# Inverse square roots of all norms: one power on GpSimd in the place of Newton's steps on VectorE

## The chip, the cores and the metric

The kernel runs on one core of one Trainium2 chip. The metric is the device time of one execution in microseconds; a kernel's time is the median of its runs. A profiled execution gives a trace of every instruction on the core's engines: TensorE (PE; its weight loads are PEld), VectorE (DVE), ScalarE (ACT), GpSimd (POOL) and the queue of SyncE (SP) that issues the transfers.

## The reference

One decoder block on x of shape (8, 224, 512) in float32, with a context of shape (8, 750, 384): self-attention, cross-attention and a quantised FFN, each followed by a residual sum and a layernorm.

```python
x = layernorm(x + attn(x)); x = layernorm(x + xattn(x, ctx)); x = layernorm(x + ffn(x))

# layernorm, eps = 1e-5, no weights
(x - mean) / sqrt(var + eps)

# attn: RMS norm of x, then 16 heads of 64; q and k each normalised per head
x = x * rsqrt(mean(x * x) + eps) * norm_w
q, k, v = x @ Wq, *split(x @ Wkv)
q = q / max(norm(q), 1e-12) * (q_gamma + 1) * 8          # k in the same way
sim = tanh(q @ k.T / 50) * 50 / 8
out = softmax(sim) @ v @ Wo

# xattn: plain attention, scale 1/8, bias bo behind Wo
# ffn: rows of x and of silu(gate) * up rounded to 8 bits, weights rounded to -1, 0, 1
```

Every inverse square root in it belongs to a norm: the RMS norm (one value for each row of x), the head norms (16 values for each row: 8 heads of q and 8 of k, for one half of the heads), and the three layernorms (one value for each row).

## The kernel before

The 1792 rows of x are 14 tiles of 128 rows, which stay in SBUF (`x[i]`) and are changed in place. On TensorE, VectorE, ScalarE and GpSimd the instructions run in the order in which the code issues them; an instruction that waits holds up all that are behind it on its engine, and the engines wait for one another through semaphores.

*Self-attention* (lines 212 to 454). It runs over 64 units, one for each of 8 batches and 8 pairs of heads. A unit issues `self_scores` (scores on TensorE, L331; tanh and exponential on ScalarE, L339 and L345; the row sums of the probabilities on GpSimd, L350 and L351, tile asm), then `self_values` of the unit before (products with v, L360; the sums spread by a matmul with ones, L369; reciprocal L377 and product L379 on VectorE), then the jobs of its slot, then the layernorm of a tile whose output projection `self_finish` ended in the unit before. The jobs prepare the batch that comes next: `project_qk` (matmuls L245; ScalarE copies the result out with the RMS norm's factor, L257; GpSimd squares it, L259; VectorE sums the squares of each head, L260), `transpose_qk`, `project_v`, `transpose_xn`. With the second of q and k, `project_qk` clips the sums (L266), calls `rsqrt` on 16 columns (tile h_rs) and multiplies q and k by it (L271). `layernorm` takes the statistics of a tile (L147 to L149), calls `rsqrt` on one column (ln_rs) and normalises (L161). `transpose_xn` turns x for the next projections: TensorE L235, then VectorE L237 (tile xnT). The PSUM buffers of tag mm are four, and L237 and L287 empty them for the next transposes and projections.

*Cross-attention* (lines 516 to 900). 64 units again. VectorE subtracts the maxima (L767), ScalarE takes the exponential (L775), GpSimd adds up the rows (L777 to L779, tiles csh and csm). `cross_add` puts the result into x[i] and takes the statistics; `roots(i0, i1)` calls `rsqrt` for a range of tiles (ln_rss) at units 34 and 57, and `normalise_x` uses them from the next unit on.

*FFN* (lines 904 to 1075). Tile by tile: `gate_up` on TensorE (L922), h on VectorE (L932), quantisation of h by ScalarE, GpSimd (L965) and VectorE (L974), a transposing transfer, `contract` on TensorE (L1010, tile dn), `add` on VectorE (L1024) with statistics. `add` calls `roots` when the last tile of one of the `groups` (L1019) has been added; `store` then normalises the tiles of the group (L1036), on GpSimd inside the loop and on VectorE behind it, and sends each out. For the three tiles left over from cross-attention, `roots(NX - 3, NX)` is called at i = 1 and `normalise_x` at i = 2.

`rsqrt` (L130) takes a first guess by a shift and a subtraction on the bits of the float (L133, L136) and improves it by three of Newton's steps of three instructions each (L140 to L142): 11 VectorE instructions on a tile of 128 rows and 1 to 16 columns.

Of the kernel before, what the change touches and what calls it, by code (L numbers as in the profile page):

```python
# [20 lines left out]
F32 = mybir.dt.float32  # L21
BF16 = mybir.dt.bfloat16
AF = mybir.ActivationFunctionType
ALU = mybir.AluOpType
AX = mybir.AxisListType
I32 = mybir.dt.int32
PSUM = bass.MemoryType.PSUM
ENGINES = {
    mybir.EngineType.PE,
# [10 lines left out]
P = 128  # L40
# [3 lines left out]
NX = B * S // P  # L44
# [19 lines left out]
def decoder_block(ctx: ExitStack, tc: tile.TileContext, a: dict, out: bass.AP):  # L64
    nc = tc.nc

    const = ctx.enter_context(tc.tile_pool(name="const", bufs=1))
# [3 lines left out]
    stat = ctx.enter_context(tc.tile_pool(name="stat", bufs=4))  # L71
# [50 lines left out]
    make_identity(nc, ident)  # L122
    ident16 = const.tile([P, P], BF16, name="ident16")
    nc.vector.tensor_copy(ident16, ident)
    ones = const.tile([P, P], F32, name="ones")
    nc.gpsimd.memset(ones, 1.0)

    gscale = const.tile([P, 2, NPAIR, 1], F32, name="gscale")

    def rsqrt(y, v, tag):  # L130

        t = stat.tile(list(v.shape), F32, tag=f"rsq{tag}", name="rsq")
        nc.vector.tensor_scalar(  # L133
            t.bitcast(I32), v.bitcast(I32), 1, None, ALU.arith_shift_right
        )
        nc.vector.tensor_scalar(  # L136
            y.bitcast(I32), t.bitcast(I32), -1, 0x5F3759DF, ALU.mult, ALU.add
        )
        for _ in range(3):
            nc.vector.tensor_tensor(t, y, y, ALU.mult)  # L140
            nc.vector.scalar_tensor_tensor(t, t, -0.5, v, ALU.mult, ALU.mult)
            nc.vector.scalar_tensor_tensor(y, t, 1.5, y, ALU.add, ALU.mult)  # L142

    def statistics(y, mv, ve):

        st = stat.tile([P, 6], F32, name="ln_st")
        nc.vector.bn_stats(st, y)  # L147
        nc.vector.bn_aggr(mv, st)
        nc.vector.tensor_scalar(ve, mv[:, 1:2], LN_EPS, None, ALU.add)  # L149

    def layernorm(tiles):

        n = len(tiles)
        mv = stat.tile([P, n, 2], F32, tag=f"ln_mv{n}", name="ln_mv")
        ve = stat.tile([P, n, 1], F32, tag=f"ln_ve{n}", name="ln_ve")
        rs = stat.tile([P, n, 1], F32, tag=f"ln_rs{n}", name="ln_rs")
        for j, i in enumerate(tiles):
            statistics(x[i], mv[:, j, :], ve[:, j, :])
        rsqrt(rs[:, :, 0], ve[:, :, 0], str(n))
        for j, i in enumerate(tiles):  # L160
            nc.vector.tensor_scalar(  # L161
                x[i], x[i], mv[:, j, 0:1], rs[:, j, :], ALU.subtract, ALU.mult
            )
# [48 lines left out]
    with tc.tile_pool(name="a_sb", bufs=2) as sb, tc.tile_pool(  # L212
        name="a_mm", bufs=4, space=PSUM
    ) as ps_mm, tc.tile_pool(name="a_sc", bufs=1, space=PSUM) as ps_sc, tc.tile_pool(
        name="a_ov", bufs=2, space=PSUM
    ) as ps_ov, tc.manual_schedule(engines=ENGINES):
        xnT = {}
        rms = stat.tile([P, NX], F32, name="rms", bufs=1)
        rms_rs = stat.tile([P, NX], F32, name="rms_rs", bufs=1)
        qkT, v, raw, norms, outs = {}, {}, {}, {}, {}  # L220
# [5 lines left out]
        def rms_norms(i0, i1):  # L226
            r = rms[:, i0:i1]
            nc.vector.tensor_scalar(r, r, 1.0 / DIM, RMS_EPS, ALU.mult, ALU.add)
            rsqrt(rms_rs[:, i0:i1], r, f"rms{i0}")


        def transpose_xn(i):
# [8 lines left out]
        def project_qk(i, which, c):  # L241

            mm = ps_mm.tile([P, 512], F32, tag="mm", name="mm_qk")
            for k in range(KD):
                nc.tensor.matmul(  # L245
                    mm,
                    lhsT=xnT[i][:, k, :],
                    rhs=(wq, wk)[which][:, k, c * 512 : (c + 1) * 512],
                    start=(k == 0),
                    stop=(k == KD - 1),  # L250
                )
            if which == 0:
                norms[i, c] = stat.tile([P, HEADS, 1], F32, name="h_ss")
            hs = norms[i, c][:, :, 0]
            qk = sb.tile([P, 512], F32, name="qk", bufs=4)
            raw[i, which, c] = qk
            nc.scalar.activation(qk, mm, AF.Identity, scale=rms_rs[:, i : i + 1])  # L257
            sq = sb.tile([P, 512], F32, tag="sq_h", name="sq_h")
            nc.gpsimd.tensor_tensor(sq, qk, qk, ALU.mult)  # L259
            nc.vector.tensor_reduce(  # L260
                hs[:, which * 8 : (which + 1) * 8],
                sq.rearrange("p (h d) -> p h d", d=DH), AX.X, ALU.add,
            )
            if which == 1:

                nc.vector.tensor_scalar(hs, hs, 1e-24, None, ALU.max)  # L266
                hr = stat.tile([P, HEADS, 1], F32, name="h_rs")
                rsqrt(hr[:, :, 0], hs, "h")
                for g in range(2):
                    part = raw[i, g, c].rearrange("p (h d) -> p h d", d=DH)  # L270
                    nc.vector.tensor_tensor(  # L271
                        part, part,
                        hr[:, g * 8 : (g + 1) * 8, :].to_broadcast([P, 8, DH]),
                        ALU.mult,
                    )
# [105 lines left out]
        def block(h):  # L381

            b, c = divmod(h, 2)
            tiles = list(needs[b])
            jobs = [(8, project_qk, i, which, c) for i in tiles for which in range(2)]
            vals = [(8, project_v, i, c) for i in tiles]
            turned = [(1, transpose_qk, i, which, c) for i in tiles for which in range(2)]
            ahead = []
            if c == 1 and b + 1 < B:
                ahead = [(1, transpose_xn, i) for i in needs[b + 1]]  # L390
            if len(tiles) == 2:
                return jobs + turned[:2] + vals[:1] + ahead + vals[1:] + turned[2:]
            return jobs + vals[:1] + ahead + vals[1:] + turned
# [4 lines left out]
        for h in range(1, 2 * B):  # L398
            jobs = block(h)
            total, at = sum(j[0] for j in jobs), 0  # L400
            for j in jobs:
                n = 4 * h - 5 + 4 * (2 * at + j[0]) // (2 * total)
# [16 lines left out]
        for i in needs[0]:  # L419
            square(i)  # L420
        rms_norms(0, 2)
        nc.vector.tensor_scalar(gscale, gam, 1.0, DH**0.5, ALU.add, ALU.mult)
        squares = list(range(2, NX))
        for n, (_, f, *args) in enumerate(block(0)):
            f(*args)
            if n < 4:
                for _ in range((1, 1, 2, 1)[n]):
                    square(squares.pop(0))
        rms_norms(2, NX // 2)
        oT = sb.tile([P, NPAIR, 2 * S], F32, name="oT", bufs=1)  # L430
        last, due = None, []
# [20 lines left out]
        for i in completes[B - 1]:  # L452
            self_finish(i)
        layernorm(due)


# [16 lines left out]
    ln_ve = const.tile([P, NX, 1], F32, name="ln_ves")  # L473
    ln_rs = const.tile([P, NX, 1], F32, name="ln_rss")
# [4 lines left out]
    xqTs = {}  # L479

    def roots(i0, i1):
        rsqrt(ln_rs[:, i0:i1, 0], ln_ve[:, i0:i1, 0], f"c{i0}")

    def normalise_x(i):

# [30 lines left out]
    with tc.tile_pool(name="c_sb", bufs=2, reuse_waits="tile") as sb, tc.tile_pool(  # L516
        name="c_mm", bufs=7, space=PSUM, reuse_waits="tile"
    ) as ps_mm, tc.tile_pool(
        name="c_ov", bufs=1, space=PSUM, reuse_waits="tile"
# [304 lines left out]
        for n, i0, i1 in ((4 * NPAIR + 2, 0, 7), (7 * NPAIR + 1, 7, NX - 3)):  # L824
            norm_at[n] = (roots, i0, i1)
            for i in range(i0, i1):
                norm_at[n + 1 + i - i0] = (normalise_x, i)
            norm_at[n + 1 + i1 - i0] = (row_scales, i0, i1)
# [75 lines left out]
    with tc.tile_pool(name="f_sb", bufs=2, reuse_waits="tile") as sb, tc.tile_pool(  # L904
        name="f_mm", bufs=6, space=PSUM, reuse_waits="tile"
    ) as ps_mm, tc.tile_pool(
        name="f_dn", bufs=2, space=PSUM, reuse_waits="tile"
    ) as ps_dn, tc.manual_schedule(engines=ENGINES):
        hs, mhs, hqs, dns, deqs = {}, {}, {}, {}, {}
        NC = HID // 512  # L910
        END = NX - 1
# [104 lines left out]
                )  # L1016


        groups = ((0, 6), (6, 9), (9, 12), (12, NX))  # L1019
        ready = []  # L1020

        def add(i):
            _, deq = deqs.pop(i)
            nc.vector.scalar_tensor_tensor(  # L1024
                x[i], dns.pop(i), deq, x[i], ALU.mult, ALU.add
            )
            statistics(x[i], ln_mv[:, i, :], ln_ve[:, i, :])
            for i0, i1 in groups:
                if i == i1 - 1:
                    roots(i0, i1)  # L1030
                    ready.extend(range(i0, i1))
# [13 lines left out]
        for i in range(NX):  # L1045
            for c in range(NC):
                gate_up(i, c)
                if c == 0 and i + 2 < NX:
                    quantise_x(i + 2)
                if c == 1 and i - LAG - 1 >= 0:  # L1050
                    add(i - LAG - 1)
                if c == 2 and i >= 1:
                    round_h(i - 1)
                    quantise_h(i - 1)
                    store(nc.gpsimd, 3 if i > 10 else 2)
            scale_h(i)
            if i - LAG >= 0:
                contract(i - LAG)
            if i == 1:
                roots(NX - 3, NX)  # L1060
            if i == 2:
                for t in range(NX - 3, NX):
                    normalise_x(t)
                row_scales(NX - 3, NX)
# [56 lines left out]
```

## Time and profile before

| what | us |
|---|---|
| runs: median of 3 (lowest, highest) | 1777.36 (1776.96, 1780.74) |
| the profiled execution | 1775.66 |
| its span, first to last instruction | 1773.8 |
| TensorE busy | 1744.9 |
| VectorE busy | 1285.6 |
| ScalarE busy | 853.4 |
| GpSimd busy | 618.1 |
| VectorE in `rsqrt`: 0 to 620 us, 620 to 1620, 1620 to the end | 99.6, 9.5, 10.1 |

Self-attention takes the first 596 us of the span, cross-attention lasts to about 1616 us, the FFN to the end. In a line of the timeline the columns are start and duration in us, engine, line of the code, operation, the tile written and the tiles read, the form, and how many instructions were merged; in brackets stands how long the engine was idle before it and what ended that. In a group of the page the numbers behind the bar are busy time in us and the mean of one instruction in ns, then the idle time before them and its releasers.

### The profile page before, as it was taken

The numbers are of one execution on the slowest core, as the hardware profiler recorded it, in microseconds if no ns is written. First come the engines' busy times: TensorE is split into PE (matmuls) and PEld (weight loads), VectorE is DVE, ScalarE is ACT, GpSimd is POOL, SyncE is SP. The second block draws the span as 40 slices with busy tenths as digits, with TensorE's granted clock in tenths as the row PEclk, the third lists the DMA queues.
The fourth block names the chain that finished last, engine by engine and source line by source line (L and its number), as shares of the span: only waits on it lengthen the run. The fifth ranks groups of instructions, "written<-read, shape, count | busy, mean of one in ns | idle before, by whom it ended". The sixth has DMA issues, their size and how long they took to land.

```text
span 1773.8 us, 24390 instructions
## 1 busy us (share of the span) xinstructions
PE 1744.9 (98%) x8994; PEld 1097.4 (62%) x8994; DVE 1285.6 (72%) x2868; ACT 853.4 (48%) x1408; POOL 618.1 (35%) x611
## 2 busy tenths in 40 slices
PE   8999999999999999999999999999999999999997
PEld 4544445444444677777677677677777776774443
DVE  4757666666666477777688688698776776986988
ACT  3344333233344266465466466365444454445663
POOL 2322322222323144344344344344434244443143
PEclk9999999999999999999999999999999999999999
DMA  7000000000004222220122112011000000031443
GB/s 279 1 1 0 1 1 1 1 1 1 1 1 145 96 72 98 72 72 33 37 66 68 45 64 84 15 42 39 1 1 30 4 1 27 1 122 43 74 81 99
DMA packets 60967, 80.52 MB, mean 45 GB/s; under 512 B 36784, under 2 KB 36784, under 8 KB 58416
## 3 DMA queue, kind: packets, MB, share of 16 engines
q1 hardware_dynamic: 60848, 78.97, 14.1%
q8 instruction: 71, 1.16, 0.3%
q14 instruction: 48, 0.39, 0.1%
HBM read 60.34 MB, written 9.96 MB: 40 GB/s over the span
## 4 chain that ended last, share of the span: by engine, by line
PE 86%; DVE 10%; issue 2%; ACT 1%; POOL 1%; DMA 1%; SPq 0%; DVEq 0%; POOLq 0%; ACTq 0%
PE mm_k L654 13%; PE mm_v L642 13%; PE mm_qk L245 11%; PE sc_c L691 8%; PE ov_c L787 8%; PE mm_o L201 5%; PE mm_co L201 5%; PE mm_q L667 5%; PE mm_f L922 4%; PE mm_v L298 3%; PE sc_a L331 3%; PE ov_a L360 2%; PE dn L1010 2%; PE ov_a L369 1%; PE tr_qk L281 1%
## 5 line engine op out<-in xcount | busy, mean ns | idle before, releaser
L777 POOL TENSOR_TENSOR csh<-cpT 125x672 f32<-125x672 f32 x128 | 207.2, 1619 | 605.5 <-DVE cpT L767 586.5
L775 ACT ACTIVATE cpT<-cpT 125x1344 f32<-125x1344 f32 x128 | 169.7, 1327 | 235.6 <-DVE cpT L767 226.9
L642 PE MATMUL mm_v<-xattn_Wv,cT 128*125 128x256 f32 x1152 | 259.1, 379 | 0.0
L654 PE MATMUL mm_k<-cT,xattn_Wk 128*128 128x375 f32 x768 | 258.6, 486 | 0.3 <-DMA cT<-ctxT 0.3
L642 PEld LDWEIGHTS mm_v<-xattn_Wv,cT 128*125 128x125 f32 x1152 | 216.3, 188 | 28.8
L699 ACT COPY cpT<-sc_c 125x448 f32<-125x448 f32 x384 | 173.9, 560 | 101.6 <-PE sc_c L691 101.3
L654 PEld LDWEIGHTS mm_k<-cT,xattn_Wk 128*128 128x128 f32 x768 | 140.0, 189 | 99.9 <-issue 12.8
L767 DVE TENSOR_TENSOR cpT<-cpT,mx_b 125x1344 f32<-125x1344 f32 x128 | 193.2, 1550 | 2.2
L701 DVE TENSOR_TENSOR cm<-sc_c,cpT 125x448 f32<-125x448 f32 x128 | 74.0, 620 | 138.4 <-ACT cpT L699 138.2
L691 PE MATMUL sc_c<-cqT,ckT 64*125 64x224 f32 x1536 | 164.3, 358 | 0.8 <-DVE cqT L675 0.7
L787 PE MATMUL ov_c<-cpT,cv 125*64 125x224 f32 x1536 | 159.4, 357 | 0.0
L691 PEld LDWEIGHTS sc_c<-cqT,ckT 64*125 64x125 f32 x1536 | 140.8, 184 | 26.4 <-ACT ckT L661 14.1
L787 PEld LDWEIGHTS ov_c<-cpT,cv 125*64 125x64 f32 x1536 | 104.6, 137 | 47.3 <-issue 18.2
L350 POOL COPY asm<-pr 32x448 f32<-32x448 f32 x64 | 35.8, 559 | 274.1 <-ACT pr L345 264.7
L260 DVE TENSOR_REDUCE h_ss<-sq_h 128x8 f32<-128x512 f32 x56 | 38.3, 684 | 121.7 <-POOL sq_h L259 121.7
L377 DVE RECIPROCAL rc_a<-ov_a 128x224 f32<-128x224 f32 x64 | 99.3, 1552 | 35.1 <-PE ov_a L369 35.1
L661 ACT COPY ckT<-mm_k 128x375 f32<-128x375 f32 x128 | 59.3, 464 | 124.1 <-PE mm_k L654 124.1
L339 ACT ACTIVATE pr<-sc_a 128x448 f32<-128x448 f32 (+1 forms) x128 | 62.2, 538 | 106.3 <-PE sc_a L331 105.8
L257 ACT ACTIVATE qk<-mm_qk,rms_rs 128x512 f32<-128x512 f32 x56 | 38.5, 688 | 153.7 <-PE mm_qk L245 150.7
L667 PE MATMUL mm_q<-xT,xattn_Wq 128*128 128x224 f32 x512 | 107.1, 352 | 0.0
L667 PEld LDWEIGHTS mm_q<-xT,xattn_Wq 128*128 128x128 f32 x512 | 96.7, 189 | 16.3
L245 PE MATMUL mm_qk<-wq,xnT 128*128 128x512 f32 x224 | 105.4, 614 | 0.8 <-DVE xnT L237 0.6
(140 smaller groups left out, 2855.4 us busy)
## 6 DMA issues: line engine op xcount, KB each, us to landing
cT<-ctxT SPq DMA_DIRECT2D x8, 1125.0 KB, 5.5
w_stage<-w_gateT SPq DMA_DIRECT2D x8, 1024.0 KB, 5.1
w_stage<-w_upT SPq DMA_DIRECT2D x8, 1024.0 KB, 5.3
w_stage<-w_downT SPq DMA_DIRECT2D x8, 1024.0 KB, 5.4
tern<-w_t SPq DMA_DIRECT2D x24, 256.0 KB, 2.1
ternary<-tern SPq DMA_DIRECT2D x3, 2048.0 KB, 12.0
x<-x SPq DMA_DIRECT2D x14, 256.0 KB, 7.9
out<-x SPq DMA_DIRECT2D x14, 256.0 KB, 2.2
```

The lines of the kernel that those rows point to most:

```text
L201: nc.tensor.matmul(mm[row : row + m, :], lhsT=oT[:, k, at : at + m], rhs=w[:, k, :], start=(k == 0), stop=(k == NPAIR - 1),)
L245: nc.tensor.matmul(mm, lhsT=xnT[i][:, k, :], rhs=(wq, wk)[which][:, k, c * 512 : (c + 1) * 512], start=(k == 0), stop=(k == KD - 1),)
L377: nc.vector.reciprocal(rc, ov[:, 1, :S])
L642: nc.tensor.matmul(mm[:, i, :], lhsT=cT[:, k, c * CT : (c + 1) * CT], rhs=xwv[:, k, g * VN : (g + 1) * VN], start=(k == 0), stop=(k == KC ...
L654: nc.tensor.matmul(mm, lhsT=xwk[:, k, hp * P : (hp + 1) * P], rhs=cT[:, k, c * HALF : (c + 1) * HALF], start=(k == 0), stop=(k == KC - 1),)
L667: nc.tensor.matmul(mm, lhsT=xwq[:, k, hp * P : (hp + 1) * P], rhs=xT[:, k, :], start=(k == 0), stop=(k == KD - 1),)
L691: nc.tensor.matmul(sc[j][:, i, :], lhsT=kT[h0 : h0 + DH, ct * CT : (ct + 1) * CT], rhs=qT[h0 : h0 + DH, :], start=True, stop=True,)
L699: nc.scalar.copy(pT[:, j, 2 * c2 : 2 * c2 + 2, :], sc[j])
L767: nc.vector.tensor_tensor(pT[:, j], pT[:, j], nm[:CT, j] .rearrange("p (o q) -> p o q", o=1) .to_broadcast([CT, NCT, S]), ALU.add,)
L775: nc.scalar.activation(pT[:, j], pT[:, j], AF.Exp)
L777: nc.gpsimd.tensor_tensor(half, pT[:, j, 0:3], pT[:, j, 3:6], ALU.add)
L787: nc.tensor.matmul(ov[h0 : h0 + DH, :], lhsT=v[:, ct, hq * DH : (hq + 1) * DH], rhs=pT[:, j, ct, :], start=(ct == 0), stop=(ct == NCT - 1),)
```

## The change

`rsqrt` becomes one instruction: GpSimd raises the values to the power -0.5, which it reads from a new constant tile `mhalf` of one column. All its callers stay where they are in the code, so each call now sits in GpSimd's queue, at the same place of the program. The scratch tile of Newton's steps falls away. In the FFN the last group of tiles, 12 and 13, becomes two groups of one tile (`END` is 13); both are still normalised by the same call of `store`, after both have been added.

```diff
+    mhalf = const.tile([P, 1], F32, name="mhalf")
+    nc.gpsimd.memset(mhalf, -0.5)
...
-    def rsqrt(y, v, tag):
-
-        t = stat.tile(list(v.shape), F32, tag=f"rsq{tag}", name="rsq")
-        nc.vector.tensor_scalar(
-            t.bitcast(I32), v.bitcast(I32), 1, None, ALU.arith_shift_right
-        )
-        nc.vector.tensor_scalar(
-            y.bitcast(I32), t.bitcast(I32), -1, 0x5F3759DF, ALU.mult, ALU.add
-        )
-        for _ in range(3):
-            nc.vector.tensor_tensor(t, y, y, ALU.mult)
-            nc.vector.scalar_tensor_tensor(t, t, -0.5, v, ALU.mult, ALU.mult)
-            nc.vector.scalar_tensor_tensor(y, t, 1.5, y, ALU.add, ALU.mult)
+    def rsqrt(y, v):
+
+        nc.gpsimd.tensor_tensor(
+            y, v, mhalf.to_broadcast([P, v.shape[-1]]), ALU.pow
+        )
...
-        groups = ((0, 6), (6, 9), (9, 12), (12, NX))
+        groups = ((0, 6), (6, 9), (9, 12), (12, END), (END, NX))
```

The other lines of the diff drop the tag from the calls of `rsqrt`.

## The prediction, made before the changed kernel was run

> **What bounds the kernel now.** I read the page first, then TensorE's waits, then the timeline around each of those waits, then the end.
>
> The page, busy shares and slices of the span:
>
> ```profile
> PE 1744.9 (98%) x8994; PEld 1097.4 (62%) x8994; DVE 1285.6 (72%) x2868; ACT 853.4 (48%) x1408; POOL 618.1 (35%) x611
> ...
> PE   8999999999999999999999999999999999999997
> ```
>
> TensorE is busy for all but 28.9 us of the span of 1773.8 us. Whatever the change frees on VectorE or loads on GpSimd is worth only what it does to those 28.9 us, or to new holes beside them. The waits of TensorE (us in total, times, longest):
>
> ```profile
> PE tr_qk L281 <- DVE xnT L237: 8.7, 3, 3.2
> ...
> PE ov_a L369 <- POOL asm L351: 1.9, 5, 0.6
> ...
> PE mm_f L922 <- DVE h L932: 0.8, 1, 0.8
> ```
>
> The first 4.25 us are waits for x and Wq; 9.35 us lie behind the last matmul; 8.73 us are three holes in self-attention, all of one kind, and two more of 0.28 and 0.29 us (at 212.7 and 506.2 us) wait for the same tile. Timeline of the third hole:
>
> ```profile
> 419.21 0.17 DVE L266 TENSOR_SCALAR h_ss<-h_ss 128x16 f32<-128x16 f32 x1
> ...
> 421.79 1.29 DVE L271 TENSOR_TENSOR qk<-qk,h_rs 128x512 f32<-128x512 f32 x2
> ...
> 425.14 0.15 DVE L149 TENSOR_SCALAR ln_ve<-ln_mv 128x1 f32<-128x1 f32 x1
> ...
> 426.18 0.98 DVE L142 SCALAR_TENSOR_TENSOR ln_rs<-rsq,ln_rs 128x1 f32<-128x1 f32 x1
> ...
> 428.37 0.55 DVE L161 TENSOR_SCALAR x<-x,ln_mv,ln_rs 128x512 f32<-128x512 f32 x1
> ...
> 430.72 1.28 DVE L237 TENSOR_TENSOR xnT<-tr_x,norm_w 128x512 f32<-128x512 f32 x2
> 431.46 0.66 PE L281 MATMUL tr_qk<-ident,qk 128*128 128x128 f32 x4 [2.98 <-DVE xnT L237]
> ```
>
> VectorE runs without a gap from 418.49 us to the hole. In that run it holds two inverse roots: the head norm's, 2.41 us (419.38 to 421.79), and the layernorm's, 3.08 us (425.29 to 428.37), where one step took 0.98 us instead of 0.16 while GpSimd ran L351. Without them L237 would come 5.5 us sooner.
>
> The end:
>
> ```profile
> 1757.82 6.64 PE L1010 MATMUL dn<-ternary,hqT 128*128 128x512 bf16 x30
> ...
> 1767.36 0.15 DVE L149 TENSOR_SCALAR ln_ves<-ln_mvs 128x1 f32<-128x1 f32 x1
> 1767.55 0.17 DVE L133 TENSOR_SCALAR rsq<-ln_ves 128x2 int32<-128x2 int32 x1
> ...
> 1769.72 1.00 DVE L1036 TENSOR_SCALAR x<-x,ln_mvs,ln_rss 128x512 f32<-128x512 f32 x2
> ```
>
> TensorE ends at 1764.46 us. VectorE adds tile 13 only from 1765.64, because it is late by then; 2.2 us of root and both normalisations stand between the last statistics and 1770.72.
>
> **The change part by part.** Removed: 50 calls (28 head norms, 12 in the layernorms of self-attention, 7 in `roots`, 3 RMS) of 11 VectorE instructions each, 119 us of VectorE by the windows of tile rsq. Added: 51 powers on GpSimd, and one memset (a row of 128x1 has 0.10 us, in a queue that then idles 11 us: nothing).
>
> The trace has no power. By size, GpSimd's rows are:
>
> ```profile
> L777 POOL TENSOR_TENSOR csh<-cpT 125x672 f32<-125x672 f32 x128 | 207.2, 1619 | 605.5 <-DVE cpT L767 586.5 <-DVE cqT L675 13.9
> L778 POOL TENSOR_TENSOR csm<-csh 125x224 f32<-125x224 f32 x128 | 93.4, 729 | 10.0
> ```
>
> With L779 (667 ns) the two small forms average 698 ns, so a column costs (1619-698)/448 = 2.06 ns and an instruction 698-224x2.06 = 0.24 us. The two-operation L1036 (2079 ns on 512 columns) costs about 4 ns a column: the columns pay for each operation. Lower bound for sixteen columns: one operation, 0.24+16x0.002 = 0.27 us. Upper bound: the eleven steps one after the other as GpSimd instructions, 11x0.27 = 3.0 us (one column: 11x0.24 = 2.65). I take a logarithm, a product and an exponential as 30 operations, an estimate from the 2 ns: 60 ns a column, so 1.2 us for sixteen columns and 0.3 us for one. It is one instruction, so it is nearer to the low row. Hand-overs: VectorE to GpSimd 0.10 us (L142 ends 1709.73, L1036 starts 1709.83), back 0.04 us (sq_h ends 122.85, L260 starts 122.89); 0.15 us together.
>
> *Head norms.* VectorE waits p+0.15 us in place of 2.40, p being the sixteen-column power; behind it in its queue wait L271, L287 and the reciprocal. On GpSimd the power stands behind its own sq_h and before the next unit's L350. Where that L350 came early (72.83 us, root waiting since 72.98), the power goes first and the row sums move from 74.64 to about 76.1; their matmul L369 comes at about 77.9. So 1.7 us of cover are left; it is gone at p of about 2.9, and then some ten such units pay the excess each.
>
> *Layernorms.* q+0.15 in place of 2.17 to 3.30 us, q being the one-column power. The unit's own row sums come before it in GpSimd's queue and are done (in the hole's unit L351 ends at 415.08 us; the L350 of 425.38 belongs to the next unit and goes behind the power).
>
> *Holes.* Each hole shrinks by what its two roots lose: 3.21 us (136.1) with roots of 2.40 and 3.30; 2.54 (349.0) with 2.41 and 2.17; 2.98 (431.5) with 2.40 and 3.08. What is left is p+q-2.19, p+q-1.74 and p+q-2.20 us. With p+q = 1.5 all three close, and so do the two small ones: 9.3 us. Behind the first hole TensorE also ran slower: eight sc_a took 1.86 us instead of 1.03 and eight ov_a 1.72 instead of 0.98, with a granted clock of 0.88 over those 14 us. 1.6 us more.
>
> *Cross-attention.* At units 34 and 57 VectorE does not need the root before the next unit, so it waits for nothing and saves about 5 us each (1155.51 to 1160.6, slowed by GpSimd's sums). TensorE's holes there (0.37 at 1170.8, 0.33 at 1529.8 <- cqT) close: 0.7 us.
>
> *FFN.* `roots(11,14)` at 1635.99 to 1638.48 is not waited for either, L932 comes 2.4 us sooner, and the hole of 0.83 us closes. For (0,6) and (6,9) the root and the normalisation are both on GpSimd; L965 queues behind it by 0.1+0.6 us, but L974 on VectorE ended 1.9 us after it (1711.14 against 1709.21) and comes sooner.
>
> *End.* VectorE is on time, so tile 13 is added at 1764.6, when TensorE hands over, not 1765.64; its statistics end at 1766.5. Tile 12's root ran beside that, and its normalisation (0.5 us) covers tile 13's power (0.15+0.3): last store ready at 1767.5 instead of 1770.7. 3.2 us. The two output transfers follow as now.
>
> Sum: 9.3+1.6+0.7+0.8+3.2 = 15.6 us. From the profiled execution's 1775.66 us (1.86 around the span) 1760.1; the median of the runs is 1.7 us above that execution: 1761.8, so 1762.
>
> One rule speaks against this. The Trainium skill, GPSIMD Engine Reference, Key points: "For elementwise work, the DVE is structurally ~2× faster." Twice VectorE's 0.174 us for eleven steps would be 3.8 us, an estimate from that page; the sum by it is that of the third case below. No power in this trace tests it.
>
> **The rivals.**
> A, the forecast: 1762, and 1758 to 1766 with p+q between 0.5 and 2.3. For it: both roots lie in the unbroken VectorE run before each hole. Chance 0.50.
>
> B, the holes do not close: the power takes 2 to 2.5 us on sixteen columns, or other work ends last in the holes' place: at the first one ScalarE is busy with v and a square until 135.3 us before it can take the next tanh. Half of 9.3+1.6 is lost and 1 us of the end: about 1769, 1766 to 1773.8. For it: L369 already waits for row sums five times. Against: the exponentials of a unit are first read in the next one, several us later. 0.20.
>
> C, slower: GpSimd works the power off step by step, p = 3.0, q = 2.65, as the upper bound. Place: the same VectorE run. The holes become 3.46, 3.91, 3.45 and about 1.7 twice, 14.2 in place of 9.3; ten row sums pay 0.1 each; two more slow restarts of 1.6 us; against that 0.7+0.8 stay and 0.9 of the end (1766.5+0.15+2.65+0.5 = 1769.8). +4.9+1.0+3.2-2.4 = +6.7: 1784, 1775 to 1790. It decides from p+q of about 5, where the holes have grown back past 9.3 us. 0.15.
>
> D, the cores take their sixteen partitions one by one: 0.06x16 = 0.96 us a column, p = 15.6. 28 times 15.75-2.4 less 3 us of slack: 290 us slower, about 2067. No row shows such a form; 0.10.
>
> E, the gains of the end and the losses of the middle cancel (p+q near 5): 1777. 0.05.
>
> **How the numbers follow.** Time 1762, the likeliest case. Range 1757 to 1786: it leaves out D (0.10), the top of C (0.04) and a little below A. A's own range is 1758 to 1766. About 0.2%, 3.6 us, is what a measurement can tell from no change. Faster: A and B, less 0.01 at B's edge, 0.69; same: E, that edge and 0.01 of C, 0.07; slower: 0.24.
>
> **What would show it.** A GpSimd row of the power on 128x16 near 1.2 us and on 128x1 near 0.3; the wait tr_qk <- xnT gone; VectorE's busy time down by some 119 us; last normalisation within 3.2 us of the last matmul. Wrong it is if L271 waits more than 2.4 us for GpSimd, if L369's wait for the row sums grows beyond a few us, or if TensorE's holes stay with another engine named.

## The result, and the profile after

| | before | after |
|---|---|---|
| median of runs, us (lowest to highest, runs) | 1778.02 (1776.96 to 1781.77, 10) | 1774.22 (1773.25 to 1775.59, 10) |
| the profiled execution, us | 1775.66 | 1775.02 |
| its span, us | 1773.8 | 1773.2 |

The ratio is 0.9974, with a 95% interval of 0.9965 to 0.9983: 3.8 us by the medians (up to 6.2 by the interval) where 15.6 were forecast. The profiled execution of before lies 2.4 us below its median and that of after 0.8 us above, so the two traces differ by 0.6 us only. The sums over traces below end at that 0.6. Line numbers of the changed kernel are 7 lower than those of before (L264 is the old L271, L344 the old L351).

The page of the changed kernel, busy shares:

```profile
PE 1745.8 (98%) x8980; PEld 1096.7 (62%) x8994; DVE 1166.2 (66%) x2318; ACT 853.0 (48%) x1408; POOL 724.4 (41%) x663
```

VectorE is 119.4 us less busy, just as counted. GpSimd is 106.3 us busier, where some 42 would have followed from the forecast's prices (28 powers of 1.2 us and 23 smaller ones of 0.3 to 0.6). TensorE still has 27.4 us of holes (28.9 before). The changed kernel's GpSimd groups by form say why:

```profile
L133 POOL TENSOR_TENSOR h_rs<-h_ss,mhalf 128x16 f32<-128x16 f32 x28 | 81.2, 2901 | 28.3 <-DVE h_ss L259 28.3
L133 POOL TENSOR_TENSOR ln_rs<-ln_ve,mhalf 128x1 f32<-128x1 f32 x11 | 6.1, 552 | 29.5 <-DVE ln_ve L142 29.5
...
L133 POOL TENSOR_TENSOR rms_rs<-rms,mhalf 128x7 f32<-128x7 f32 x1 | 1.5, 1479 | 1.5 <-DVE rms L221 1.5
```

The power takes 2.90 us on sixteen columns and 0.55 on one: (2.901-0.552)/15 = 0.157 us a column and 0.40 fixed, by which seven columns take 1.49 (measured 1.48). TensorE's waits in the changed kernel (us in total, times, longest):

```profile
PE ov_a L362 <- POOL asm L344: 6.2, 8, 2.8
...
PE tr_x L228 <- DVE qT L280: 2.7, 4, 0.7
PE tr_qk L274 <- DVE xnT L230: 2.7, 3, 0.9
```

The wait for xnT that set the three large holes has gone from 8.7 to 2.7 us. The wait for the row sums has gone from 1.9 to 6.2, one of its eight times being 2.8 us, and `tr_x <- qT` is new. The third hole, in the timeline of the changed kernel:

```profile
425.59 2.90 POOL L133 TENSOR_TENSOR h_rs<-h_ss,mhalf 128x16 f32<-128x16 f32 x1 [1.01 <-DVE h_ss L259]
...
428.52 1.29 DVE L264 TENSOR_TENSOR qk<-qk,h_rs 128x512 f32<-128x512 f32 x2 [3.01 <-POOL h_rs L133]
...
430.48 0.66 PE L228 MATMUL tr_x<-ident,x 128*128 128x128 f32 x4 [0.66 <-DVE qT L280]
...
432.10 0.55 POOL L133 TENSOR_TENSOR ln_rs<-ln_ve,mhalf 128x1 f32<-128x1 f32 x1 [3.61 <-DVE ln_ve L142]
...
432.69 0.87 DVE L154 TENSOR_SCALAR x<-x,ln_mv,ln_rs 128x512 f32<-128x512 f32 x1 [0.67 <-POOL ln_rs L133]
...
436.10 0.66 PE L274 MATMUL tr_qk<-ident,qk 128*128 128x128 f32 x4 [0.88 <-DVE xnT L230]
```

The layernorm's root now costs VectorE 0.67 us instead of 3.08. The head norm's costs 3.01 instead of 2.41: VectorE stands idle while GpSimd works, and for longer than it took itself. The hole is 0.66+0.88 = 1.54 us where it was 2.98.

The stretch in which the longest wait for row sums arose, in the timeline of the changed kernel:

```profile
150.91 2.90 POOL L133 TENSOR_TENSOR h_rs<-h_ss,mhalf 128x16 f32<-128x16 f32 x1 [1.01 <-DVE h_ss L259]
...
153.85 1.29 DVE L264 TENSOR_TENSOR qk<-qk,h_rs 128x512 f32<-128x512 f32 x2 [3.02 <-POOL h_rs L133]
...
155.06 0.17 DVE L221 TENSOR_SCALAR rms<-rms 128x7 f32<-128x7 f32 x1
...
155.30 1.48 POOL L133 TENSOR_TENSOR rms_rs<-rms,mhalf 128x7 f32<-128x7 f32 x1 [1.49 <-DVE rms L221]
156.84 0.55 POOL L343 COPY asm<-pr 32x448 f32<-32x448 f32 x1
157.48 1.12 POOL L344 TENSOR_TENSOR asm<-pr 96x448 f32<-96x448 f32 x1
...
158.65 1.01 PE L362 MATMUL ov_a<-asm,ones 128*64 128x224 f32 x4 [2.85 <-POOL asm L344]
...
159.60 6.29 PE L238 MATMUL mm_qk<-wk,xnT 128*128 128x512 f32 x8
```

The same place in the timeline of before:

```profile
150.41 0.56 POOL L350 COPY asm<-pr 32x448 f32<-32x448 f32 x1 [0.93 <-ACT pr L345]
...
151.04 1.16 POOL L351 TENSOR_TENSOR asm<-pr 96x448 f32<-96x448 f32 x1
...
155.21 0.55 PE L369 MATMUL ov_a<-asm,ones 128*64 128x224 f32 x4
...
155.69 3.70 PE L245 MATMUL mm_qk<-wk,xnT 128*128 128x512 f32 x8
```

There the row sums of this unit ran from 150.41 to 152.20 us, and L369 read them at 155.21 without waiting. In the changed kernel GpSimd first works off the head power, then stands 1.49 us before the RMS power, whose input VectorE delivers only behind L264, which itself waited for the head power. The row sums stand behind both. They end at 158.60, and TensorE waits 2.85 us. The eight mm_qk behind it take 6.29 us instead of 3.70. The stretches of 2 us there (us from and length; busy TensorE, weight load, VectorE, ScalarE, GpSimd; granted clock, 1.00 being TensorE's full clock and 0.50 half of it; share of the DMA engines; GB/s):

```profile
158.00:160.00 2.00, 1.35 (x5) 0.70 (x6) 0.37 (x1) 0.00 (x0) 1.76 (x3) 0.50 0.04 8
160.00:162.00 2.00, 2.00 (x3) 0.77 (x3) 1.97 (x3) 0.00 (x0) 1.52 (x2) 0.50 0.00 0
162.00:164.00 2.00, 2.00 (x3) 0.68 (x2) 0.21 (x1) 0.00 (x0) 0.00 (x0) 0.50 0.00 0
164.00:166.00 2.00, 2.00 (x7) 0.94 (x6) 0.00 (x0) 0.08 (x1) 0.00 (x0) 0.79 0.00 0
```

The granted clock was 0.50 for 6.83 us, from 158.02 us in the wait on. The wait and this stretch together cost 6.1 us, the shift of the same instructions from before to after.

The end, in the timeline of the changed kernel:

```profile
1759.46 7.07 PE L1003 MATMUL dn<-ternary,hqT 128*128 128x512 bf16 x31
...
1766.57 0.75 DVE L1017 SCALAR_TENSOR_TENSOR x<-dn,deq,x 128x512 f32<-128x512 f32 x1 [0.74 <-PE dn L1003]
...
1768.53 0.79 POOL L133 TENSOR_TENSOR ln_rss<-ln_ves,mhalf 128x1 f32<-128x1 f32 x1 [2.07 <-DVE ln_ves L142]
1769.35 0.55 DVE L1029 TENSOR_SCALAR x<-x,ln_mvs,ln_rss 128x512 f32<-128x512 f32 x1 [0.45 <-POOL ln_rss L133]
```

VectorE takes the last tile as TensorE ends, and the last normalisation is done 1769.90-1766.53 = 3.4 us behind the last matmul (6.3 before).

How far the same matmuls moved from the one trace to the other, place by place (plus is later):

| place | forecast, us | measured, us |
|---|---|---|
| up to 90 us | 0 | +3.7 |
| three large holes, with the slow stretch behind the first | -10.3 | -5.3 |
| the two small holes | -0.6 | +1.1 |
| row sums behind the RMS power, at 155 us | 0 | +6.1 |
| row sums at 449 us | 0 | +1.0 |
| rest of self-attention (what is left to its end) | 0 | -0.4 |
| cross-attention | -0.7 | -2.4 |
| FFN up to its last matmul | -0.8 | -1.7 |
| end | -3.2 | -2.7 |
| sum | -15.6 | -0.6 |

Of the +3.7 at the start, 1.6 are there by 31 us and cannot be told from the spread between executions: the first tr_qk begins at 22.13 us in before, at 23.46 in after, and at 22.62 and 24.18 in two kernels below that have before's code there. Two steps of 1.0 and 0.9 us are the head powers'. They stand at these waits of the changed kernel:

```profile
58.49 0.66 PE L228 MATMUL tr_x<-ident,x 128*128 128x128 f32 x4 [0.70 <-DVE qT L280]
...
81.45 0.60 PE L362 MATMUL ov_a<-asm,ones 128*64 128x224 f32 x4 [0.73 <-POOL asm L344]
```

All four kernels with whole head powers (after, and three of those below) have both steps in their traces, and the three with Newton's steps in the head norms have neither.

### The profile page after: what moved, and what is told of

The parts are those of the page before. It is cut to its first block, busy times and chain, and to the rows that moved or that the text cites. A ratio compares the mean times of both kernels' runs of the same rounds, so it can differ in the third digit from the quotient of the medians.

```text
span 1773.2 us, 23866 instructions
## 1 busy us (share of the span) xinstructions
PE 1745.8 (98%) x8980; PEld 1096.7 (62%) x8994; DVE 1166.2 (66%) x2318; ACT 853.0 (48%) x1408; POOL 724.4 (41%) x663
## 4 chain that ended last, share of the span: by engine, by line
PE 90%; POOL 4%; DVE 3%; issue 1%; ACT 1%; DMA 0%; POOLq 0%; SPq 0%; DVEq 0%; ACTq 0%
PE mm_k L647 14%; PE mm_v L635 14%; PE mm_qk L238 10%; PE sc_c L684 9%; PE ov_c L780 9%; PE mm_o L194 5%; PE mm_q L660 5%; PE mm_co L194 5%; PE mm_f L915 5%; PE mm_v L291 3%; PE sc_a L324 3%; PE ov_a L353 2%; PE dn L1003 2%; POOL h_rs L133 2%; PE ov_a L362 1%
## 5 line engine op out<-in xcount | busy, mean ns | idle before, releaser
L635 PEld LDWEIGHTS mm_v<-xattn_Wv,cT 128*125 128x125 f32 x1152 | 216.2, 188 | 28.9
L238 PE MATMUL mm_qk<-wk,xnT 128*128 128x512 f32 x224 | 104.8, 612 | 0.0
```

The source lines that it names most:

```text
L238: nc.tensor.matmul(mm, lhsT=xnT[i][:, k, :], rhs=(wq, wk)[which][:, k, c * 512 : (c + 1) * 512], start=(k == 0), stop=(k == KD - 1),)
L635: nc.tensor.matmul(mm[:, i, :], lhsT=cT[:, k, c * CT : (c + 1) * CT], rhs=xwv[:, k, g * VN : (g + 1) * VN], start=(k == 0), stop=(k == KC ...
```

## The experiments

Two theories stood against each other. H: the head norms' powers are the loss, since a power of 2.90 us is longer than Newton's 2.40 and VectorE does nothing beside it. R: the RMS power in front of the row sums is the loss. Each kernel was also timed against before on its own chip (medians of 1779.4 and 1779.0 us).

**Head norms back on VectorE** (all other roots stay powers; `newton` is before's `rsqrt`).

```diff
-                rsqrt(hr[:, :, 0], hs)
+                newton(hr[:, :, 0], hs, "h")
```

> The changed kernel with the 28 head norms back on VectorE by Newton's steps; RMS, layernorms, roots and the split of the last group stay on GpSimd. Theory H (the head norm's power, 2.90 us on 16 columns in the trace after, is longer than the 2.40 us it replaces, and this is what ate the gain of self-attention): self-attention ends some 8 us before that of the kernel before instead of 6.1 us behind it, the time falls by 12 to 15 us against the changed kernel, to 1760 to 1763 us. Rival R (the loss is one place, where the RMS power of seven columns, 1.48 us, stands ahead of row sums in GpSimd's queue and L362 waits 2.85 us): that place stays, about 1768 us or above.

1766.15 us (1765.01 to 1767.92); ratio 0.9927, 0.9911 to 0.9943. It falls between the two: most of the loss is the head norms', but not all. The row sums still wait, by TensorE's waits in this kernel (L378 is before's L369):

```profile
PE ov_a L378 <- POOL asm L360: 4.1, 6, 2.2
```

Behind the wait of 2.2 us the clock was 0.5 for 3.41 us, and this place alone cost 4.1 us in this trace.

**Only the head norms as powers**, all else as before.

```diff
-        rsqrt(rs[:, :, 0], ve[:, :, 0], str(n))
+        newton(rs[:, :, 0], ve[:, :, 0], str(n))
...
-                rsqrt(hr[:, :, 0], hs, "h")
+                rsqrt(hr[:, :, 0], hs)
```

> The kernel before with the head norms alone as a power on GpSimd; everything else by Newton's steps, the last group unsplit. Theory H: slower than before by 5 to 10 us (3.05 us in place of 2.41 in each head norm, the five holes each longer by 0.6 us, row sums late behind the power): 1783 to 1788 us. Rival R: within 2 us of before, 1776 to 1780 us, as the RMS power is not there.

1789.59 us (1783.74 to 1790.86); ratio 1.0050, 1.0031 to 1.0069. The head norms' part of the change makes the kernel slower, by 9 us by the ratio. TensorE's waits in it:

```profile
PE tr_qk L290 <- DVE xnT L246: 7.8, 3, 3.0
...
PE ov_a L378 <- POOL asm L360: 4.0, 8, 0.7
PE tr_x L244 <- DVE qT L296: 3.0, 4, 0.9
```

The holes are nearly back, the row sums wait twice as long as in before (4.0 against 1.9) but never over 0.7 us, and `tr_x <- qT` is there: it belongs to the head norms. Not all of the 9 us are the waits themselves. This trace has three stretches of 3.41 us at half clock, one behind each hole, where before's trace has one; at about 1.7 us each the two more are worth 3.4 us.

**RMS roots back on VectorE** (all else as after).

```diff
-        rsqrt(rms_rs[:, i0:i1], r)
+        newton(rms_rs[:, i0:i1], r, f"rms{i0}")
```

> The changed kernel with the three RMS roots alone back on VectorE. Rival R: the wait of 2.85 us at L362 and the 2.7 us by which the eight matmuls behind it were slow go, 5.5 us against the changed kernel, 1768 to 1769 us, and nothing else is wrong in self-attention. Theory H: less, 1 to 4 us, because VectorE takes the root (2 us) in the same place and the head power still holds the row sums back.

1770.18 us (1769.93 to 1770.95); ratio 0.9949, 0.9933 to 0.9964, so 4.0 us below after by the medians; the two intervals lie side by side without overlapping (0.9964 and 0.9965). The wait of 2.85 us is gone (the row sums' longest is 0.7), and no stretch of this trace has a clock of 0.5. The RMS power had a part in the loss, which the first experiment had left open; at 4 us it is the smaller one.

**The head power in two halves.** Each half takes eight columns and starts right behind the sums of q or k, so that q's root is taken while k is still on its way, and q is multiplied while GpSimd takes k's root (the tile h_rs is now made with q).

```diff
+            own = slice(which * 8, (which + 1) * 8)
+            nc.vector.tensor_scalar(hs[:, own], hs[:, own], 1e-24, None, ALU.max)
+            rsqrt(hr[:, own, 0], hs[:, own])
...
-                nc.vector.tensor_scalar(hs, hs, 1e-24, None, ALU.max)
-                rsqrt(hr[:, :, 0], hs)
```

> The changed kernel with each head norm's power cut in two of eight columns, q's eight taken as soon as q's squares are summed, k's eight behind k's. From the trace after (0.55 us for one column, 2.90 for sixteen: 0.157 us a column, 0.39 fixed) each is 1.65 us, so VectorE waits about 1.8 us instead of 3.05 behind k's sums. Theory H: the holes of self-attention close as with a p of 1.65, 7 to 11 us against the changed kernel, 1763 to 1767 us. Rival R: no more than 2 us, 1772 us or above, since the place of the RMS power stays.

1760.88 us (1759.18 to 1761.07); ratio 0.9892, 0.9873 to 0.9912. Better than either theory had it. Its timeline:

```profile
146.15 0.69 DVE L265 TENSOR_TENSOR qk<-qk,h_rs 128x512 f32<-128x512 f32 x1
146.32 2.01 POOL L133 TENSOR_TENSOR h_rs<-h_ss,mhalf 128x8 f32<-128x8 f32 x1 [1.00 <-DVE h_ss L259]
...
148.36 0.69 DVE L265 TENSOR_TENSOR qk<-qk,h_rs 128x512 f32<-128x512 f32 x1 [1.53 <-POOL h_rs L133]
...
152.57 0.60 PE L363 MATMUL ov_a<-asm,ones 128*64 128x224 f32 x4 [1.65 <-POOL asm L345]
153.10 3.40 PE L238 MATMUL mm_qk<-wk,xnT 128*128 128x512 f32 x4
```

VectorE multiplies q while GpSimd works on k's root, and idles 1.53 us instead of 3.01. With that the holes close nearly as forecast: against before, -3.0 at the first (and -1.6 in the slow stretch behind it), -2.05 at the second, -2.8 at the third. What is left is the RMS power ahead of the row sums, with 1.65 us of wait and a half clock behind it (four mm_qk in 3.40 us).

**The same, with the RMS power out of the way.** The call for the second half of the tiles is moved from the slot at 155 us to a later one.

```diff
-                if not squares:
-                    rms_norms(NX // 2, NX)
+            if n == 13:
+                rms_norms(NX // 2, NX)
```

> e4_halves with the RMS power of tiles 7 to 13 called two units later, behind unit 13 in place of unit 11; it is still a power on GpSimd. Theory Q (its place in GpSimd's queue costs, between a head norm's power and the row sums of the next unit, not its 1.48 us): the wait of 1.65 us at L363 and the slow matmuls behind it go, some 3.5 us against e4_halves, 1757 to 1758 us. Rival (GpSimd has too much work in self-attention): the loss appears elsewhere, 1760 to 1761 us.

1758.32 us (1757.11 to 1759.46); ratio 0.9884, 0.9866 to 0.9901: the fastest of all, 20.7 us below before on its chip. Its interval overlaps that of the halves alone, and the two were timed on different chips, so the 2.6 us between them rest on the trace:

```profile
PE ov_a L363 <- POOL asm L345: 1.8, 5, 0.5
...
PE tr_qk L275 <- DVE xnT L230: 0.8, 3, 0.5
```

Theory Q of the expectation holds. Row sums wait as in before (1.9, longest 0.6), xnT holds TensorE for 0.8 us instead of 8.7, and the clock was full up to the last matmul.

**Only the roots of cross-attention and FFN**, with the split of the last group; all of self-attention as before.

```diff
-        rsqrt(ln_rs[:, i0:i1, 0], ln_ve[:, i0:i1, 0], f"c{i0}")
+        rsqrt(ln_rs[:, i0:i1, 0], ln_ve[:, i0:i1, 0])
...
-        groups = ((0, 6), (6, 9), (9, 12), (12, NX))
+        groups = ((0, 6), (6, 9), (9, 12), (12, END), (END, NX))
```

> The changed kernel with head norms, RMS and the layernorms of self-attention back on VectorE by Newton's steps: only the roots of cross-attention and of the FFN, and the split of the last group, are left of the change. Theory: these parts are what gained (1.2 and 1.1 us at the two roots of cross-attention, 1.9 in the FFN, 2.7 at the end, from the drift of the traces): 6 to 8 us below the kernel before. Rival: the end and the FFN are bound by TensorE alone, 2 to 3 us below it.

1773.96 us (1769.56 to 1774.96); ratio 0.9969, 0.9956 to 0.9983, 5.1 us by the medians. That is below the 6 to 8 expected. In the trace the difference was lost in self-attention, where the code is before's own: it has three stretches at half clock, two of 3.41 us and one of 6.83, where before's has one. One of them, in the windows of this kernel:

```profile
353.00:355.00 2.00, 2.00 (x14) 1.05 (x12) 0.00 (x0) 1.50 (x4) 0.00 (x0) 0.66 0.00 0
```

Between 120 and 450 us this trace fell 4.4 us further behind before's.

**The same, and the layernorms of self-attention** as powers; head norms and RMS roots by Newton.

```diff
-        newton(rs[:, :, 0], ve[:, :, 0], str(n))
+        rsqrt(rs[:, :, 0], ve[:, :, 0])
```

> As e6_roots_only, but the layernorms of self-attention are powers on GpSimd, so it is e1_heads_newton with the RMS roots on VectorE too. Theory: it has the gain of e6_roots_only and that of the layernorms in the holes (each root 0.70 us in place of 2.17 to 3.30, in front of five holes of 9.3 us in all): 5 to 9 us below e6_roots_only, and 3 to 4 us below e1_heads_newton, about 1762 us. Rival (the holes close only if the head norm is shortened as well): within 2 us of e6_roots_only.

1762.37 us (1760.76 to 1764.48); ratio 0.9908, 0.9894 to 0.9922. As expected in time. The layernorms' share is 11.6 us, more than the 5 to 9 foreseen. With the smaller holes (1.3 us at most) the half-clock stretches of the run before went too, some 6.8 us (1.7 for each 3.41). This trace has one other, at 25 us, behind a wait of 2.44 us for the first head norm, where the code is before's. So 28 head powers and three RMS powers spoil most of what the other, smaller powers bring.

**The last group unsplit.**

```diff
-        groups = ((0, 6), (6, 9), (9, 12), (12, END), (END, NX))
+        groups = ((0, 6), (6, 9), (9, 12), (12, NX))
```

> The changed kernel with the last two tiles in one group again. Theory: the split is worth what one normalisation covers of a power, 0.5 to 0.8 us: within 0.1% of the changed kernel, 1774 to 1776 us. Rival (the split brings most of the 2.7 us at the end): 2 to 3 us slower than it.

1775.39 us (1772.53 to 1776.38); ratio 0.9980, 0.9971 to 0.9989. Against after's 0.9974 nothing can be told by the time. In the traces the stretch from the last statistics to the end of the last normalisation is 1.81 us unsplit and 1.45 split: the split is worth about 0.4 us. Up to the FFN this is the changed kernel's own code, and TensorE waits 2.85 us for the row sums again; here 3.41 us at half clock followed instead of 6.83, and the place cost 4.7 us instead of 6.1.

## Why the prediction was wrong

**The mechanism held.** "Each hole shrinks by what its two roots lose." With the measured p = 2.90 and q = 0.55, the three formulas give 1.26, 1.71 and 1.25 us; 1.54, 1.55 and 1.54 were measured (0.66 as a wait of tr_x for qT, the rest as the wait for xnT). The kernel whose wait for the head root is 1.53 us instead of 3.01 closes the holes almost fully.

**The step that failed is the price of the power.** "I take a logarithm, a product and an exponential as 30 operations ... 60 ns a column, so 1.2 us for sixteen columns ... It is one instruction, so it is nearer to the low row." It took 157 ns a column, 2.90 us for sixteen. The 2.06 ns of one operation came from rows; the count of 30 came from none, and no run shows it. The measured column is worth 76 of them. The upper bound of 3.0 was almost reached there, while one column took 0.55 and not 2.65. Neither bound had both a fixed part and a large part per column. So the case is none of A to C: p is C's, q is near A's, and their sum of 3.45 leaves about half of the three holes, which is what B foresaw from a shorter power. It cost 6.7 us of the forecast: 5.0 in the large holes and 1.7 in the small ones, where TensorE now waits 0.66 us each for qT. The estimate of 3.8 us from the Trainium skill, GPSIMD Engine Reference, Key points, that was set beside it was nearer than 1.2. It prices Newton's eleven steps, though, and the one power of 2.90 us lies below it.

**A root that was not costed.** The sum counted the RMS roots but placed none of them. The one at 155 us stands in GpSimd's queue between a head power and a unit's row sums, and its input hangs on VectorE's L264, which hangs on that same head power. That is 6.1 us in the two traces, and 4.7 in the trace of the unsplit kernel, where the half clock behind the same wait was shorter. With Newton's RMS roots and whole head powers the place still moves by 1.0 us, which is the head power's part. Taking the RMS powers out gained 4.0 us by the medians with the head powers whole. Moving that one call later gained 2.6 with them halved, where 1.65 us of the wait was left.

**The cover of the row sums.** It was said to be gone "at p of about 2.9, and then some ten such units pay the excess each". p came to 2.90, and with the head powers alone eight waits make 4.0 us where five made 1.9. That was right in kind and small in size: two such waits, at 78 and 449 us, moved TensorE by 0.9 and 1.0 us.

**The head norm's own wait.** It was named as the sign of an error if "L271 waits more than 2.4 us for GpSimd"; it waits 3.01, 28 times. The kernel with only the head norms changed shows the price: 9 us slower. Part of it is `tr_x <- qT`, which was not foreseen. L287 stands behind L271 in VectorE's queue, and the PSUM buffers that it empties are the next tr_x's.

**What was right.** VectorE's 119 us. Cross-attention and FFN wait for no root, and gained 4.1 us where 1.5 were counted. Each hole closed, and in cross-attention the 24 sc_c behind each took 2.54 us instead of 3.16. The end gained 2.7 of 3.2 us; the last power took 0.79 us beside a normalisation, instead of 0.3.

With what the holes really gave, 4.2 instead of 10.9 us, the sum would have been 8.9. The RMS power (6.1), the start (3.7) and the row sums at 449 us (1.0) take more than that in the two traces; the larger gains of cross-attention and FFN leave 0.6. Of the start's 3.7 us, 1.9 are the head powers', another cost of them that the sum left out.

## What to carry to other kernels

An operation that no row shows can have both a fixed price and a price per column: bound both, and where one of them decides, cost the edit at the high end. When work moves to another engine, read what stands behind it in that engine's queue and whether its input comes from the engine that is waiting for it; here the place of one such power cost 6.1 us in one trace and 4.7 in another. If a wide operation must be moved, cut it so that the first part runs while the rest of its input is still being made: the halved head power turned a 0.3% gain into 1.1%.

## What the runs showed of the hardware

**Short waits can be followed by a half clock.** The granted clock in these traces is 1.0 or 0.5 (values between are means over a window), and up to the last matmul 0.5 comes in stretches of 3.41 or 6.83 us; one of 3.41 costs about 1.7 us. In the ten traces TensorE waits 15 times for 1.65 us or longer after its first matmuls. Twelve of these waits have such a stretch beside them, which begins between 0.7 us before the wait's end and 1.8 us after it, and no stretch stands anywhere else; none of the four waits of 1.0 to 1.4 us has one. The length of the wait does not decide: 1.65 us brought a stretch in the kernel with halves, holes of 2.54 and 2.98 us brought none in before, and holes of 2.52 and 2.98 at the same places brought one each in the kernel with only the later roots changed. The Trainium skill, TensorE: Matmul & The Clock Gate, section What's actually happening, has a free-running window of 4096 cycles, 3413 ns, and half rate after an idle one. The length and the 0.5 agree. A wait of 1.65 us is no whole idle window, and the same page's advice (Why this matters for your kernels) to keep gaps under about 3 us was not enough here. The measurement decides. That the waits bring the stretches is read from where both stand; no run changed a wait alone. In these traces a wait of 1.65 us or more cost its own length and, in most cases, 1.7 us or more on top.

**The end of a power can start a collision.** It releases VectorE's L264 and GpSimd's next instruction at once. In the changed kernel the pair of L264 took 2.12 us at 21.89 us and 2.49 at 47.11, beside sq_h and the row sums' copy, and 1.29 at 428.52 and 153.85 us, where GpSimd was idle. The Trainium skill, SBUF — State Buffer, section Who interferes with whom, says that a VectorE instruction with two inputs in SBUF contends with a GpSimd instruction that reads SBUF; these rows agree. On the whole the change did not make these collisions worse: one such product takes 0.78 us on average in the changed kernel and 0.87 in before.

**The power is not slow on one column.** 0.55 us against 2.17 for Newton's eleven instructions on VectorE; on sixteen columns it is 2.90 against 2.40. By the line above (0.40 and 0.157 a column) the two would cross between 12 and 13 columns, an estimate; no run has such a width.
